# Ends of row blocks spread between messages, and GpSimd operations behind its gathers, in a two-layer graph kernel

## The chip, the cores and the metric

The kernel runs on one core of a Trainium2 chip. The metric is the device time of one execution in microseconds (us). Each core has five engines with queues of their own: TensorE (PE in the profile, its weight loads PEld), VectorE (DVE), ScalarE (ACT), GpSimd (POOL) and SyncE (SP), which here only issues transfers. Each engine runs its queue in order.

## The reference

The input is a feature matrix `x` (2708 x 128), an adjacency matrix `adj` (2708 x 2708, mostly zeros, rows normalised), and small weights. Two layers follow each other, each as `x = layernorm(x + layer(x))`.

```python
# layer 0, cut to what matters
XW = mobius_matvec(W, x)                      # x @ W, rescaled per row
gamma = 2 / max(1 - |XW|^2, eps)
two_mean = (adj @ (gamma * XW)) / (adj @ (gamma - 1))
# ... scalings per row, relu, then x = layernorm(x + ...)

# layer 1
s = x @ msg_w[:, :D].T
d = x @ msg_w[:, D:].T
messages = gelu(s[:, None, :] + d[None, :, :] + msg_b)
aggregated = einsum('ijd,ij->id', messages, adj)
new = concat([x, aggregated]) @ upd_w.T + upd_b
h = gelu(new) + x
x = layernorm(x + layernorm(h) * ln_w + ln_b)
```

## The kernel before, in words

The rows are cut into 22 blocks of 128. Layer 0 reads `adj` block by block, multiplies it on TensorE (L324), and finds at the same time where each row has its nonzero entries: ScalarE takes signs (L319), TensorE and VectorE turn them into keys and lists (L350, L358, `extract`). The nonzero entries of all rows of a block are packed into tiles of 128 edges: 99 tiles over 25 lists (block 0 has four). For each tile, one indirect transfer issued by GpSimd gathers the 128 values of `adj` into a column of `V` (L452, through the helper at L191). Its list of addresses `F` comes from a pool with three buffers (L430), written by VectorE at L448.

After layer 0, `layer0_end` computes the new `x` for blocks 0 to 15 and then 16 to 21, and writes the product `d` of layer 1 into a table in device memory (L535).

Layer 1 works only on the edges. For a tile of 128 edges, `messages` issues one indirect transfer that gathers 128 rows of the table (L651, again L191), repeats the row's `s` with a matmul against a selection matrix `R` (L652), builds `rv`, a 128x128 matrix with the values of `V` at each edge's row, on VectorE (L654), adds (L657), applies gelu on ScalarE (L658), and multiplies by `rv` on TensorE into the sum of the block (L660). Up to four tiles form a quad, which shares one buffer `dd` (a ring of seven) and one of three buffers `rv`.

Tiles are "early" if all their rows lie in the first 16 blocks of the table, and otherwise "late"; 62 are early (`soon`), 37 late. For blocks 0 to 7 the early tiles go first, as far as they fit into the ring, then into the buffer `aT` that layer 0 no longer needs; their sums are kept. Then all blocks follow in five groups, `GROUPS = [(0, 8), (8, 6), (14, 4), (18, 2), (20, 2)]`, with the remaining tiles. Each block ends with a copy of its sum (L702) and `update` (three or four matmuls into `sel` and a gelu, L610 to L614). After a group's last block, `finish` takes the whole group: add of `x1` (L618), statistics of each block (L594, L595), inverse root (L224 to L229 on VectorE, or one pow on GpSimd at L604 for the last group), scaling on ScalarE (L627), two wide VectorE operations (L628, L629), statistics again, scaling on ScalarE (L635) and a store for each block (L637).

The order of instructions within each engine is set by a planner, from the order of the program, dependences, and hints: `tc.issue_after(ins)` asks that what stands under it be put behind an instruction.

Of the kernel before, what the change touches and what calls it, by code (L numbers as in the profile page):

```python
# [10 lines left out]
F32 = mybir.dt.float32  # L11
# [3 lines left out]
AF = mybir.ActivationFunctionType  # L15
OP = mybir.AluOpType
AX = mybir.AxisListType

P = 128
# [3 lines left out]
LN_EPS = 1e-5  # L23
# [5 lines left out]
EARLY = 8  # L29
# [4 lines left out]
SPLIT = 16  # L34
# [41 lines left out]
def hyperbolic_then_message_kernel(  # L76
# [22 lines left out]
    const = ctx.enter_context(tc.tile_pool(name="const", bufs=1))  # L99
# [7 lines left out]
    w0_sb, wT, rowvec, o = pk[:, :D], pk[:, D : 5 * D].rearrange("p (i d) -> p i d", d=D), {}, 5 * D  # L107
# [27 lines left out]
    iotaN = const.tile([P, P], F32, name="iotaN")  # L135
# [51 lines left out]

    of_block = {b: [l for l, v in enumerate(LISTS) if v[0] == b] for b in range(NB)}

    def gather(o, src, at):  # L190
        nc.gpsimd.indirect_dma_start(  # L191
            out=o, out_offset=None, in_=src, in_offset=bass.IndirectOffsetOnAxis(ap=at, axis=0)
        )

    mx = big.tile([P, NB, D], F32, name="mx")
    y = big.tile([P, NB, D + 2], F32, name="y")
# [15 lines left out]
    def cols(n):  # L212
        count[0] += 1
        return sc.tile([P, n], F32, name=f"c{count[0]}")
# [49 lines left out]
    edge = ctx.enter_context(tc.tile_pool(name="edge", bufs=2))  # L264
    fin = ctx.enter_context(tc.tile_pool(name="fin", bufs=2))
# [5 lines left out]
    for g, n in quads:  # L271
# [18 lines left out]
    a, th, u, v, c = (cols(NB) for _ in range(5))  # L290
# [163 lines left out]
    x1, x1T = x_sb, xT  # L454
# [85 lines left out]
    last = {}  # L540
# [38 lines left out]
    gd = nom  # L579
# [10 lines left out]
    def moments(v, n, pool):  # L590
        st = pool.tile([P, n, 6], F32, name="st1")
        mv = pool.tile([P, n, 2], F32, name="mv1")
        for k in range(n):
            nc.vector.bn_stats(st[:, k, :], v[:, k, :])  # L594
            nc.vector.bn_aggr(mv[:, k, :], st[:, k, :])  # L595
        ve = pool.tile([P, n], F32, name="ve1")
        nc.vector.tensor_scalar_add(ve, mv[:, :, 1], LN_EPS)
        return mv, ve

    def inverse_root(ve, n, pool, last):  # L600
        if not last:
# [5 lines left out]
    def update(h, k, b, ags):  # L607
        up = bank("sel", 1)
        s = slice(b * P, (b + 1) * P)
        nc.tensor.matmul(up[:, :D], lhsT=x1T[:, s], rhs=wT[:, 2, :], start=True, stop=False)  # L610
        for ag in ags:
            nc.tensor.matmul(up[:, :D], lhsT=ag, rhs=wT[:, 3, :], start=False, stop=False)  # L612
        nc.tensor.matmul(up[:, :D], lhsT=ones[0:1, :], rhs=rowvec["ub"][0:1, :], start=False, stop=True)  # L613
        nc.scalar.activation(h[:, k, :], up[:, :D], AF.Gelu)  # L614

    def finish(h, b0, n, pool, last):

        nc.vector.tensor_add(h, h, x1[:, b0 : b0 + n, :])  # L618
        mv, ve = moments(h, n, pool)
        rs = inverse_root(ve, n, pool, last)  # L620
        nb = pool.tile([P, n], F32, name="nb")
        nc.vector.scalar_tensor_tensor(nb, mv[:, :, 0], -1.0, rs, op0=OP.mult, op1=OP.mult)
        for k0 in range(0, n, 4):
            k1 = min(n, k0 + 4)
            v = h[:, k0:k1, :]
            for k in range(k0, k1):
                nc.scalar.activation(h[:, k, :], h[:, k, :], AF.Identity, scale=rs[:, k : k + 1], bias=nb[:, k : k + 1])  # L627
            nc.vector.tensor_mul(v, v, wide(rowvec["lw"], k1 - k0))  # L628
            nc.vector.tensor_add(v, v, xlb[:, b0 + k0 : b0 + k1, :D])  # L629
        mv, ve = moments(h, n, pool)  # L630
        rs = inverse_root(ve, n, pool, last)
        nb = pool.tile([P, n], F32, name="nb")
        nc.vector.scalar_tensor_tensor(nb, mv[:, :, 0], -1.0, rs, op0=OP.mult, op1=OP.mult)
        for k in range(n):
            nc.scalar.activation(h[:, k, :], h[:, k, :], AF.Identity, scale=rs[:, k : k + 1], bias=nb[:, k : k + 1])  # L635
            r = rows[b0 + k]
            nc.sync.dma_start(out[(b0 + k) * P : (b0 + k) * P + r, :], h[:r, k, :])  # L637

    def ring(w):
        return edge.tile([P, 4, P], F32, name="dd", bufs=RING)[:, :w, :]  # L640

    def messages(b, ag, tiles, first, final, bins, room=ring):

        for q, k0 in enumerate(range(0, len(tiles), 4)):
            ts = tiles[k0 : k0 + 4]
            w = len(ts)
            dd = room(w)
            X = bank(bins[q % len(bins)]).rearrange("p (t d) -> p t d", d=D)[:, :w, :]
            rv = edge.tile([P, 4, P], F32, name="rv", bufs=3)
            for k, t in enumerate(ts):  # L650
                gather(dd[:, k, :], table[: SPLIT * P] if t in soon else table, J[:, t : t + 1])  # L651
                nc.tensor.matmul(X[:, k, :], lhsT=R[:, t, :], rhs=s_nm[:, b, :], start=True, stop=True)  # L652

                nc.vector.tensor_scalar(  # L654
                    rv[:, k, :], iotaN, rid[:, t : t + 1], V[:, t : t + 1], op0=OP.is_equal, op1=OP.mult
                )
            nc.vector.tensor_tensor(dd, X, dd, op=OP.add)  # L657
            nc.scalar.activation(dd, dd, AF.Gelu)  # L658
            for k in range(w):
                nc.tensor.matmul(  # L660
                    ag[:, :P],
                    lhsT=dd[:, k, :],
                    rhs=rv[:, k, :],
                    start=(first and k0 == 0 and k == 0),
                    stop=(final and k0 + k == len(tiles) - 1),
                )

    def own(b, ag):
        nc.tensor.matmul(ag[:, :P], lhsT=gd[:, b, :D], rhs=ident, start=True, stop=False)

    early, late, soon = {}, {}, set()
# [15 lines left out]
    for b in range(EARLY):  # L687
        ag = bank("ag", 1)
# [3 lines left out]
    for g0, gn in GROUPS:  # L692
        h = gd[:, g0 : g0 + gn, :D]
        for b in range(g0, g0 + gn):
            ag = bank("mp")
            agT = edge.tile([P, P], F32, name="agT")
# [29 lines left out]
    for i, v in enumerate(seconds):  # L726
        k = v.shape[1]
# [32 lines left out]
    with tc.If(dense > 0):  # L760
        with tc.tile_pool(name="dn", bufs=1) as dn:
            room = R.rearrange("p t i -> p (t i)")
            dT, sT, agT, row = (room[:, k * NP : (k + 1) * NP] for k in range(4))
            ge = flat(mx)
            nc.vector.memset(agT, 0.0)
            for c0 in range(0, NP, 512):
                c1_ = min(NP, c0 + 512)
                dp = bank("mp")
                nc.tensor.matmul(dp[:, : c1_ - c0], lhsT=wT[:, 1, :], rhs=x1T[:, c0:c1_], start=True, stop=True)
                nc.vector.tensor_copy(dT[:, c0:c1_], dp[:, : c1_ - c0])  # L770
                sp = bank("kx")
                nc.tensor.matmul(sp[:, : c1_ - c0], lhsT=wT[:, 0, :], rhs=x1T[:, c0:c1_], start=True, stop=True)
                nc.vector.tensor_scalar_add(sT[:, c0:c1_], sp[:, : c1_ - c0], mb)
            with tc.For_i(0, N, 1) as i:
                nc.sync.dma_start(row[:, :N], adj[bass.ds(i, 1), :].to_broadcast([P, N]))
                nc.scalar.activation(ge[:, :N], dT[:, :N], AF.Gelu, bias=sT[:, bass.ds(i, 1)])
                nc.vector.tensor_mul(ge[:, :N], ge[:, :N], row[:, :N])
                nc.vector.tensor_reduce(agT[:, bass.ds(i, 1)], ge[:, :N], axis=AX.X, op=OP.add)
            for b in range(NB):
                h = dn.tile([P, 1, D], F32, name="h")  # L780
                update(h, 0, b, [agT[:, b * P : (b + 1) * P]])
                finish(h, b, 1, dn, last=False)


_INS = [
# [73 lines left out]
```

## Time and profile before

| | |
|---|---|
| median of nine runs | 389.37 us (388.19 to 392.37) |
| the profiled execution, as timed | 390.27 us |
| its span in the profile | 388.5 us |
| TensorE busy | 300.3 us, 77% |
| VectorE busy | 277.7 us, 71% |
| ScalarE busy | 208.4 us, 54% |
| GpSimd busy | 204.9 us, 53% |
| mean granted TensorE clock | 0.867 |

The median is over separate runs; every duration comes from the one profiled execution, whose time is 0.9 us above the median and 1.8 us above its own span. In the page, a line of a group gives the source line, engine, operation, output and inputs, the count, the busy time in us, the mean of one in ns, and behind the second bar the idle time of the engine just before them with what ended most of it. L191 is the line of the helper that issues every gather, for values and for table rows alike.

### The profile page before, as it was taken

How to read it: one execution, taken by the hardware profiler on the slowest of the kernel's cores; microseconds unless marked ns; L12 is line 12 of the kernel's file. 1: busy time of each engine (PE TensorE's matmuls, PEld its weight loads, DVE VectorE, ACT ScalarE, POOL GpSimd, SP SyncE). 2: the span in 40 equal slices, each digit the busy share in tenths (PEclk: the TensorE clock that was granted, in tenths of full speed). 3: DMA queues.
4: the chain of work that ended last, by engine and by line, in shares of the span. 5: the costliest groups of instructions: out<-in, count | busy, mean ns of one | idle time of the engine just before them, and what ended most of it. 6: DMA issues, size and time to landing. Idle time of an engine off the chain costs nothing.

```text
span 388.5 us, 7784 instructions
## 1 busy us (share of the span) xinstructions
PE 300.3 (77%) x2427; PEld 271.9 (70%) x2427; DVE 277.7 (71%) x1474; ACT 208.4 (54%) x562; POOL 204.9 (53%) x297
## 2 busy tenths in 40 slices
PE   2519999999999999999799820759979995976300
PEld 2418999999999999999678720559869874865200
DVE  0996988887776677799958887399734656668650
ACT  2861857677667667689348632293323252273430
POOL 7400077777777444333320777777777777771000
PEclk9956999999999999999799955769968996899555
DMA  8800744434456546544426111212221222240110
GB/s 304 353 2 2 270 163 139 177 150 151 151 189 232 178 162 225 214 150 151 149 58 201 29 36 47 73 49 56 53 56 49 57 50 47 54 107 16 42 42 12
DMA packets 16237, 45.14 MB, mean 116 GB/s; under 512 B 5626, under 2 KB 11150, under 8 KB 13374
## 3 DMA queue, kind: packets, MB, share of 16 engines
q1 hardware_dynamic: 9710, 37.43, 26.6%
q0 software_dynamic: 6336, 6.55, 7.7%
q10 hardware_dynamic: 144, 0.60, 0.5%
q8 instruction: 20, 0.33, 0.3%
q14 instruction: 27, 0.22, 0.2%
HBM read 41.74 MB, written 2.83 MB: 115 GB/s over the span
## 4 chain that ended last, share of the span: by engine, by line
PE 56%; DVE 21%; ACT 10%; DMA 6%; issue 4%; POOL 2%; DVEq 0%; POOLq 0%; ACTq 0%
PE mp L324 23%; PE sel L438 6%; PE kx L350 6%; DMA dd<-table_dram,J 3%; PE mp L660 3%; PE X L528 3%; PE X L652 3%; POOL dd L191 2%; PE sel L612 2%; ACT sgn L319 2%; PE sel L613 2%; DVE rv L654 2%; PE kx L344 2%; DMA xT<-in_x_t_dram 2%; DVE dd L657 1%
## 5 line engine op out<-in xcount | busy, mean ns | idle before, releaser
L191 POOL DMA_INDIRECT V<-in_adj_dram,F x99 | 95.7, 966 | 101.2 <-DVE top L358 31.4
L324 PE MATMUL mp<-y,aT 128*128 128x130 f32 x968 | 123.3, 282 | 0.9 <-DVE y L308 0.9
L324 PEld LDWEIGHTS mp<-y,aT 128*128 128x128 f32 x968 | 115.8, 194 | 1.4 <-DVE y L308 1.1
L191 POOL DMA_INDIRECT dd<-table_dram,J x81 | 79.3, 979 | 35.4 <-issue 19.5
L319 ACT ACTIVATE sgn<-aT 128x2816 bf16<-128x2816 f32 x22 | 56.0, 2547 | 7.7 <-ACT junk L332 7.3
L652 PE MATMUL X<-mx,R 128*128 128x128 f32 x198 | 34.6, 308 | 15.0 <-DVE dd L657 12.7
L652 PEld LDWEIGHTS X<-mx,R 128*128 128x128 f32 x198 | 29.1, 214 | 17.8 <-DVE dd L657 14.1
L350 PEld LDWEIGHTS <-sgn 128*128 128x128 bf16 x484 | 28.7, 100 | 17.5 <-issue 9.1
L350 PE MATMUL kx<-kd,sgn 128*128 128x128 bf16 x484 | 34.0, 222 | 7.5 <-ACT sgn L319 7.5
L654 DVE TENSOR_SCALAR rv<-iotaN,rid,V 128x128 f32<-128x128 f32 x99 | 30.7, 364 | 9.0 <-PE mp L660 8.3
L438 PE MATMUL sel<-z,R 128*128 128x49 f32 (+4 forms) x198 | 29.2, 284 | 6.9 <-DVE z L429 2.6
L438 PEld LDWEIGHTS sel<-z,R 128*128 128x128 f32 x198 | 26.1, 199 | 9.0 <-DVE z L429 2.8
L358 DVE MAX8 top<-kx 128x8 f32<-128x128 f32 (+3 forms) x152 | 28.6, 236 | 2.9 <-PE kx L350 2.5
L409 ACT ACTIVATE work<-iota,mid 128x512 f32<-128x512 f32 (+3 forms) x53 | 26.8, 553 | 3.7 <-DVE mid L402 3.6
L657 DVE TENSOR_TENSOR dd<-X,dd 128x384 f32<-128x384 f32 (+3 forms) x29 | 15.1, 525 | 19.1 <-DMA dd<-table_dram,J 12.4
L658 ACT ACTIVATE dd<-dd 128x384 f32<-128x384 f32 (+3 forms) x29 | 13.8, 497 | 23.8 <-DVE dd L657 21.9
L660 PE MATMUL mp<-rv,dd 128*128 128x128 f32 x116 | 21.4, 317 | 4.0 <-ACT dd L658 4.0
L441 DVE TENSOR_TENSOR work<-sel,place 128x144 f32<-128x144 f32 (+11 forms) x29 | 11.7, 404 | 16.4 <-PE sel L438 16.1
L660 PEld LDWEIGHTS mp<-rv,dd 128*128 128x128 f32 x116 | 17.3, 217 | 6.3 <-ACT dd L658 5.1
L191 POOL DMA_INDIRECT aT<-table_dram,J x18 | 17.1, 950 | 5.5 <-issue 4.6
L362 ACT ACTIVATE junk_s<-kx 128x512 bf16<-128x512 f32 (+2 forms) x25 | 14.0, 562 | 8.8 <-DVE top L358 6.8
L614 ACT ACTIVATE nom<-sel 128x128 f32<-128x128 f32 x22 | 6.0, 274 | 20.4 <-PE sel L613 20.2
(204 smaller groups left out, 569.9 us busy)
## 6 DMA issues: line engine op xcount, KB each, us to landing
aT<-in_adj_t_dram SPq DMA_DIRECT2D x22, 1408.0 KB, 6.8
V<-in_adj_dram,F POOLq DMA_INDIRECT x99
xT<-in_x_t_dram SPq DMA_DIRECT2D x2, 704.0 KB, 7.2
x_sb<-in_x_nm_dram SPq DMA_DIRECT2D x2, 704.0 KB, 8.4
out_dram<-nom SPq DMA_DIRECT2D x21, 64.0 KB, 1.8
dd<-table_dram,J POOLq DMA_INDIRECT x81
table_dram<-dt SPq DMA_DIRECT2D x5, 256.0 KB, 2.3
pk<-in_pack_dram ACTq DMA_DIRECT2D x1, 587.5 KB
```

What stands on the lines that cost most here:

```text
L191: nc.gpsimd.indirect_dma_start(out=o, out_offset=None, in_=src, in_offset=bass.IndirectOffsetOnAxis(ap=at, axis=0))
L319: nc.scalar.activation(sgn, aT, AF.Sign, accum_out=signs[:, b : b + 1])
L324: nc.tensor.matmul(op[:, : D + 2], lhsT=aT[:, j, :], rhs=y[:, j, :], start=(j == 0), stop=(j == NB - 1))
L350: nc.tensor.matmul(kp[:, i * P : (i + 1) * P], lhsT=sgn[:, j, :], rhs=kd[:, q, :], start=False, stop=(i == len(groups) - 1 and j == j1 - 1),)
L358: nc.vector.max(top[:, c : c + 8], seg[:, s, :])
L362: nc.scalar.activation(t[:, :w], kp[:, :w], AF.Sign, accum_out=poss[:, l : l + 1])
L409: nc.scalar.activation(r0, iota[:, k0 * P : k1 * P], AF.Abs, scale=2.0, bias=mid[:, k : k + 1])
L438: nc.tensor.matmul(sp[:, k, :], lhsT=R[:, t0 + k0 + k, :], rhs=z, start=True, stop=True)
L652: nc.tensor.matmul(X[:, k, :], lhsT=R[:, t, :], rhs=s_nm[:, b, :], start=True, stop=True)
L654: nc.vector.tensor_scalar(rv[:, k, :], iotaN, rid[:, t : t + 1], V[:, t : t + 1], op0=OP.is_equal, op1=OP.mult)
L657: nc.vector.tensor_tensor(dd, X, dd, op=OP.add)
L660: nc.tensor.matmul(ag[:, :P], lhsT=dd[:, k, :], rhs=rv[:, k, :], start=(first and k0 == 0 and k == 0), stop=(final and k0 + k == len(tiles ...
```

## The change

Four things are changed, in layer 1 and in the helper for gathers.

The end of a row block is cut into parts. `node`, `first` and `finish` are now generators, and `messages` calls `step` at the end of each quad, which takes every waiting block one part further. The first statistics are taken for each block as soon as it is updated (`first`), and no longer for the group.

The first norm is written as two VectorE operations for each block, each doing two steps, where ScalarE did one operation and VectorE two wide ones. In the last group the second norm's scaling is a VectorE operation too.

Behind each gather of a `V` column and of an early tile, GpSimd raises a column of ones to a constant power and writes it into a scratch column `gap`, which nothing reads.

For late tiles, GpSimd builds `rv` itself, behind the tile's gather, where VectorE did.

The diff, without the part that serves a path not taken here:

```diff
+    gap = const.tile([P, 1], F32, name="gap")
+
+    def gather(o, src, at, wait=True):
+        last = nc.gpsimd.indirect_dma_start(
             out=o, out_offset=None, in_=src, in_offset=bass.IndirectOffsetOnAxis(ap=at, axis=0)
         )
+        if wait:
+            with tc.issue_after(last.ins):
+                nc.gpsimd.tensor_tensor(gap, ones[:, :1], nhalf, op=OP.pow)
+        return last
...
     def finish(h, b0, n, pool, last):
-        nc.vector.tensor_add(h, h, x1[:, b0 : b0 + n, :])
-        mv, ve = moments(h, n, pool)
+        mv = mvs.pop(b0)
+        ve = pool.tile([P, n], F32, name="ve1")
+        nc.vector.tensor_scalar_add(ve, mv[:, :, 1], LN_EPS)
         rs = inverse_root(ve, n, pool, last)
-        nb = pool.tile([P, n], F32, name="nb")
-        nc.vector.scalar_tensor_tensor(nb, mv[:, :, 0], -1.0, rs, op0=OP.mult, op1=OP.mult)
-        for k0 in range(0, n, 4):
-            k1 = min(n, k0 + 4)
-            v = h[:, k0:k1, :]
-            for k in range(k0, k1):
-                nc.scalar.activation(h[:, k, :], h[:, k, :], AF.Identity, scale=rs[:, k : k + 1], bias=nb[:, k : k + 1])
-            nc.vector.tensor_mul(v, v, wide(rowvec["lw"], k1 - k0))
-            nc.vector.tensor_add(v, v, xlb[:, b0 + k0 : b0 + k1, :D])
-        mv, ve = moments(h, n, pool)
+        yield
+        st = pool.tile([P, n, 6], F32, name="st1")
+        mw = pool.tile([P, n, 2], F32, name="mv1")
+        for k in range(n):
+            v = h[:, k, :]
+            nc.vector.scalar_tensor_tensor(v, v, mv[:, k, 0:1], rowvec["lw"], op0=OP.subtract, op1=OP.mult)
+            nc.vector.scalar_tensor_tensor(v, v, rs[:, k : k + 1], xlb[:, b0 + k, :D], op0=OP.mult, op1=OP.add)
+            moments(h, st, mw, [k])
+            if k % 2 and k + 1 < n:
+                yield
+        ve = pool.tile([P, n], F32, name="ve1")
+        nc.vector.tensor_scalar_add(ve, mw[:, :, 1], LN_EPS)
+        yield
         rs = inverse_root(ve, n, pool, last)
...
         for k in range(n):
+            v, r = h[:, k, :], rows[b0 + k]
+            if last:
+                nc.vector.tensor_scalar(v, v, mw[:, k, 0:1], rs[:, k : k + 1], op0=OP.subtract, op1=OP.mult)
+            else:
+                nc.scalar.activation(v, v, AF.Identity, scale=rs[:, k : k + 1], bias=nb[:, k : k + 1])
             nc.sync.dma_start(out[(b0 + k) * P : (b0 + k) * P + r, :], h[:r, k, :])
...
+    def first(h, b0, n, pool, k):
+        if k == 0:
+            mvs[b0] = pool.tile([P, n, 2], F32, name="mv0")
+        st = pool.tile([P, 1, 6], F32, name="st0")
+        nc.vector.tensor_add(h[:, k, :], h[:, k, :], x1[:, b0 + k, :])
+        moments(h, st, mvs[b0], [k], k)
+
+    def node(h, k, b, b0, n, ag, more, pool):
+        agT = edge.tile([P, P], F32, name="agT")
+        nc.scalar.copy(agT, ag[:, :P])
+        yield
+        update(h, k, b, [agT, *more])
+        yield
+        first(h, b0, n, pool, k)
+        if k == n - 1:
+            yield
+            yield from finish(h, b0, n, pool, last=(b == NB - 1))
+
+    queue = []
+
+    def step():
+        for g in list(queue):
+            if next(g, queue) is queue:
+                queue.remove(g)
...
-                gather(dd[:, k, :], table[: SPLIT * P] if t in soon else table, J[:, t : t + 1])
+                g = gather(dd[:, k, :], table[: SPLIT * P] if t in soon else table, J[:, t : t + 1], t in soon)
                 nc.tensor.matmul(X[:, k, :], lhsT=R[:, t, :], rhs=s_nm[:, b, :], start=True, stop=True)
-                nc.vector.tensor_scalar(
-                    rv[:, k, :], iotaN, rid[:, t : t + 1], V[:, t : t + 1], op0=OP.is_equal, op1=OP.mult
-                )
+                args = rv[:, k, :], iotaN, rid[:, t : t + 1], V[:, t : t + 1]
+                if t in soon:
+                    nc.vector.tensor_scalar(*args, op0=OP.is_equal, op1=OP.mult)
+                else:
+                    with tc.issue_after(g.ins):
+                        nc.gpsimd.tensor_scalar(*args, op0=OP.is_equal, op1=OP.mult)
...
+            step()
...
-            nc.scalar.copy(agT, ag[:, :P])
-            update(h, b - g0, b, [agT, gd[:, b, :D]] if b < EARLY else [agT])
-        finish(h, g0, gn, fin, last=(g0 + gn == NB))
+            queue.append(node(h, b - g0, b, g0, gn, ag, [gd[:, b, :D]] if b < EARLY else [], fin))
+    while queue:
+        step()
```

More of the change, by code (lines that the diff above doesn't have):

```diff
@@ L188, in hyperbolic_then_message_kernel @@
     of_block = {b: [l for l, v in enumerate(LISTS) if v[0] == b] for b in range(NB)}
-    def gather(o, src, at):
-        nc.gpsimd.indirect_dma_start(
+    gap = const.tile([P, 1], F32, name="gap")
+    def gather(o, src, at, wait=True):
+        last = nc.gpsimd.indirect_dma_start(
             out=o, out_offset=None, in_=src, in_offset=bass.IndirectOffsetOnAxis(ap=at, axis=0)
         )
+        if wait:
+            with tc.issue_after(last.ins):
+                nc.gpsimd.tensor_tensor(gap, ones[:, :1], nhalf, op=OP.pow)
+        return last
     mx = big.tile([P, NB, D], F32, name="mx")
@@ L588, in hyperbolic_then_message_kernel, with moments @@
         nc.vector.tensor_add(xlb[:, g : g + n, :D], x1[:, g : g + n, :], wide(rowvec["lb"], n))
[L590 to L598, printed above, removed]
+    def moments(v, st, mv, ks, k0=0):
+        for k in ks:
+            nc.vector.bn_stats(st[:, k - k0, :], v[:, k, :])
+            nc.vector.bn_aggr(mv[:, k, :], st[:, k - k0, :])
     def inverse_root(ve, n, pool, last):
@@ L631, in finish @@
+        ve = pool.tile([P, n], F32, name="ve1")
+        nc.vector.tensor_scalar_add(ve, mw[:, :, 1], LN_EPS)
+        yield
         rs = inverse_root(ve, n, pool, last)
-        nb = pool.tile([P, n], F32, name="nb")
-        nc.vector.scalar_tensor_tensor(nb, mv[:, :, 0], -1.0, rs, op0=OP.mult, op1=OP.mult)
+        if not last:
+            nb = pool.tile([P, n], F32, name="nb")
+            nc.vector.scalar_tensor_tensor(nb, mw[:, :, 0], -1.0, rs, op0=OP.mult, op1=OP.mult)
         for k in range(n):
-            nc.scalar.activation(h[:, k, :], h[:, k, :], AF.Identity, scale=rs[:, k : k + 1], bias=nb[:, k : k + 1])
-            r = rows[b0 + k]
-            nc.sync.dma_start(out[(b0 + k) * P : (b0 + k) * P + r, :], h[:r, k, :])
+            v, r = h[:, k, :], rows[b0 + k]
[3 more added lines that the diff above has]
+                nc.scalar.activation(v, v, AF.Identity, scale=rs[:, k : k + 1], bias=nb[:, k : k + 1])
+            nc.sync.dma_start(out[(b0 + k) * P : (b0 + k) * P + r, :], h[:r, k, :])
@@ new lines, in finish @@
+        yield
+    mvs = {}
+    def first(h, b0, n, pool, k):
[12 more added lines that the diff above has]
+        if k == n - 1:
+            yield
+            yield from finish(h, b0, n, pool, last=(b == NB - 1))
@@ L695, in hyperbolic_then_message_kernel @@
             ag = bank("mp")
-            agT = edge.tile([P, P], F32, name="agT")
             if b < EARLY:
@@ L781, in hyperbolic_then_message_kernel @@
                 update(h, 0, b, [agT[:, b * P : (b + 1) * P]])
-                finish(h, b, 1, dn, last=False)
+                first(h, b, 1, dn, 0)
+                for _ in finish(h, b, 1, dn, last=False):
+                    pass
 _INS = [
```

## The prediction, made before the changed kernel had run

> **What bounds the kernel now.** I read the page first (slices and costliest groups), then the timeline of GpSimd, the table of stretches, and last the chain of waits of the final 15 us.
>
> The page, slices and groups:
>
> ```profile
> DVE  0996988887776677799958887399734656668650
> POOL 7400077777777444333320777777777777771000
> L191 POOL DMA_INDIRECT V<-in_adj_dram,F x99 | 95.7, 966 | 101.2 <-DVE top L358 31.4
> L191 POOL DMA_INDIRECT dd<-table_dram,J x81 | 79.3, 979 | 35.4 <-issue 19.5
> ```
>
> GpSimd shows one digit, 7, in slices 23 to 36 (213.7 to 349.7 us). A constant share below full is the sign of a fixed pitch. The timeline of GpSimd (start, duration, in brackets the idle time before) confirms it, and shows where the row of gathers ends:
>
> ```profile
> 347.62 0.95 POOL L191 DMA_INDIRECT dd<-table_dram,J  x1 [0.30 <-ACT dd L658]
> 348.87 0.94 POOL L191 DMA_INDIRECT dd<-table_dram,J  x1 [0.30 <-issue]
> 350.12 0.94 POOL L191 DMA_INDIRECT dd<-table_dram,J  x1 [0.30 <-ACT nom L614]
> 373.68 0.73 POOL L604 TENSOR_TENSOR ro<-ve,nhalf 128x2 f32<-128x2 f32 x1 [22.62 <-DVE ro L225]
> 379.31 0.70 POOL L604 TENSOR_TENSOR ro<-ve,nhalf 128x2 f32<-128x2 f32 x1 [4.89 <-DVE ve L597]
> ```
>
> A gather starts every 1.25 us (0.94 plus 0.30), whatever it moves. From 213.5 to 351.06 us there are 108 of them (9 of V, 99 of table rows) with never more than about 0.3 us between them. So GpSimd's queue sets the moment T = 351.06 us at which the last gather is issued; any GpSimd time put ahead of it moves T one for one. The span ends at 388.5: the **tail** behind T is 37.4 us. In it GpSimd and TensorE idle, and VectorE and ScalarE hand the norms to each other:
>
> ```profile
> core 0: us, PE busy (x) PEld busy (x) DVE busy (x) ACT busy (x) POOL busy (x), PEclk, DMA share, GB/s
> 345.00:355.00 10.00, 8.24 (x54) 6.59 (x53) 7.15 (x27) 5.07 (x16) 4.71 (x5) 1.00 0.25 51
> 355.00:365.00 10.00, 4.37 (x22) 3.16 (x20) 6.84 (x44) 5.11 (x16) 0.00 (x0) 0.75 0.14 41
> 365.00:375.00 10.00, 1.01 (x4) 0.93 (x4) 7.50 (x61) 2.86 (x8) 0.73 (x1) 0.50 0.10 28
> 375.00:389.00 14.00, 0.00 (x0) 0.00 (x0) 2.44 (x12) 2.52 (x6) 0.70 (x1) 0.50 0.06 18
> ```
>
> The last add of messages (L657) ends at 357.75, the last norm (L635) at 381.17; 7.3 us of stores and ending follow. So the tail is 6.7 + 23.4 + 7.3.
>
> **What the Trainium skill says.** *Perfetto Trace Analysis*, DMA Instruction — SWDGE: the end shown for a gather is when the last DSP has written its descriptors, and the DSP completes the instruction after that. That leaves open what the 0.30 us is: completion of the gather (then any operation behind it waits too), or the start of the next gather (then something else fits there). The trace has no operation directly behind a gather. The same page (GPSIMD Engine Instruction) advises timing by start-to-start spacing; the 1.25 us is such a spacing. *GPSIMD Engine Reference*, 2.1 Instruction dispatch: completion needs all eight cores, and a core goes to the next instruction once its own share is done. *SBUF — State Buffer*, Who interferes with whom: a VectorE operation with two SBUF inputs contends with a GpSimd one that reads SBUF. No slowing shows in the trace: the add of one 128x256 pair at L628 takes 0.42 to 0.43 us both at 351 us among gathers and at 371 us without.
>
> **The change, part by part.**
>
> 1. *The tail.* Norms of earlier blocks no longer stand behind each other at the end, and 22 ScalarE operations (L627, 479 ns) go. But by the built order VectorE still has 105 instructions behind its last message add, because groups 14-17, 18-19 and 20-21 finish there. By rows of before: 57 small ones at 0.10 (25 such took 2.4 us from 366.68 to 369.1) is 5.7; 12 pairs of statistics at 0.26 is 3.1; 4 adds at 0.28 is 1.1; 14 of the new two-operation norm at 0.29 (between L334, 283 ns, and L328, 345 ns) is 4.1; 2 last scalings at 0.3 is 0.6. Together 14.6, plus one pow round through GpSimd, 0.9 (379.17 to 380.04). The last data lands 2.5 to 3.75 us behind its issue, so about T+2.6 (data of four gathers in the chain of waits); the eight `rv` that GpSimd now builds behind the last gather take 8 x 0.30 = 2.4 and are there as well. End at T + 2.6 + 15.5 + 7.3 = T + 25.4 instead of T + 37.4: **-12.0**. Bounds -6 (five blocks wait for those `rv`, and TensorE needs some eight matmuls for each, 0.43 at half clock and 0.22 at full in the chain of waits, so up to 17 us instead of 9) and -16 (part of VectorE's work done while it waits).
> 2. *VectorE relieved.* 37 `rv` at 364 ns leave it, 13.5 us between 283 and 349 us. VectorE is busy 3 to 8 of every 10 us there; the gathers cover this. Counted as 0.
> 3. *GpSimd's scratch columns and `rv`.* By the built order there are, from the first row gather on, still 108 gathers, 71 scratch columns, and 29 `rv` ahead of the last gather. They stand in 56 places between gathers, 43 beginning with a scratch column and 13 with an `rv`. One place holds 24 columns: the 23 gathers issued ahead of the `aT` ones have their columns put behind the eighteenth `aT` gather, and not "behind each". Prices: an `rv` is one 128x128 two-step scalar operation, 0.30 (the page's L136). A column has no row. From below 0.09 (a one-column memset, L185); 0.19 is the one-column L148; from above 0.70 (the two-column pow, L604). I take 0.19, and that the operation lies in the 0.30:
>    - 43 places: 0.94 + 0.19 instead of 1.25, -0.11 each: -4.7 (a gain is not excluded).
>    - 13 places: 0.94 + 0.30, about 0.
>    - 23 further columns of the lump, 0.19: +4.4, with nothing to hide them.
>    - 21 further operations in runs, 16 `rv` at 0.30 and 5 columns at 0.19: +5.7.
>    - Sum on T: **+5.4**. From below, -8 (a column at 0.09); from above, with 0.30 kept and 0.70 paid, 71 x 0.70 + 29 x 0.38 = +61.
> 4. *Columns behind the 90 V gathers of layer 0.* The queue there runs full from 48 to 126 us at 1.25, then waits for VectorE. A slower pitch is covered until a buffer fails: `F` has three, so the list of block 11 writes `F` (143 us) only when the gathers of block 8 are through. Sixty-one gathers from 48 us on end at 48 + 61 x pitch: at 1.13, 117 us, cost 0; the cover is gone above a pitch of 1.55.
> 5. *New waits.* An `rv` on GpSimd waits for TensorE to release one of three buffers; gathers queue behind it. In before VectorE waited so 6 times, 8.3 us. By the order 14 gathers stand ahead of the first ten `rv`, so the release is old by then: 0, at most +8. SP's queue gets the same 22 stores.
>
> Sum: -12.0 + 5.4 = -6.6. The profiled execution took 390.27 us around its span of 388.5; that gives 383.7. It stood 0.9 us above the median of the runs shown, 389.37, so **382.8 us**, 1.7% less.
>
> **Rivals.**
>
> *The column is paid in part (slower).* If pow needs 0.5 for one column (two take 0.70) and the 0.30 only makes room for part: 43 x 0.19 + 23 x 0.5 + 16 x 0.30 + 5 x 0.5 = 27, less 12, is +15: 404. For it: pow is the only one of GpSimd's small operations with 0.7 us. It decides from about 0.3 us a column, where 43 places cost nothing won and the lump costs 7.
>
> *Paid in full (slower still).* The 0.30 belongs to the gather's own completion; pitch 0.94 + 0.30 + 0.5 = 1.74: 71 x 0.5 + 29 x 0.38 = 46, layer 0 waits for `F` until 154 us instead of 143, +11; less 12: 435. For it: the 0.30 follows every gather, with a semaphore wait or without.
>
> *A gather with another operation behind it ends sooner.* 56 gathers shorter by a further 0.30: T 17 us earlier, but TensorE is busy 85 of the 100 us from 255 to 355, so at most 14 of it: 368. Against it: a gather with 2.5 us of nothing behind it also shows 0.94.
>
> *It doesn't do what it says.* The planner already lumps 24 columns; if only the tail's -12 and a lump of like size remain, 389.
>
> **How the numbers follow.** A measurement of this kernel tells about 0.5% from no change. The columns fit: 0.40, own range 374 to 391 (0.31 faster, 0.06 same, 0.03 slower). Sooner ends: 0.20, faster. Paid in part: 0.25, 391 to 412, slower. Paid in full: 0.13, 412 to 460, slower. Nothing left: 0.02. Faster 0.51, same 0.08, slower 0.41. The range 364 to 412 leaves out the full price and the best of the sooner ends, some 0.18.
>
> **What would show it.** In the profile after: start-to-start from a gather over its column to the next gather (1.13 right, 1.25 neutral, 1.4 or more wrong); the lump of 24 (4.6 us or 12); the start of the last gather against 350.12; the time from it to the end (25 or 37); the gathers of layer 0 (end of the full stretch near 117 to 126 us, or waits of VectorE's L448). The forecast is wrong if the columns take 0.3 us or more each.

## The result, and the profile after

The changed kernel takes 471.1 us (median of 10 runs, 470.1 to 475.9), the kernel before 389.8 us (31 runs, 388.2 to 392.8): ratio **1.211**, 95% interval 1.208 to 1.215. It is slower by 81 us where 7 us less were forecast, and it lies above the stated range of 364 to 412 us. Runs that came out more than 1.5% above the fastest of their kernel are left out of the times from here on, except in the part on the two sets in which the kernel before takes 500 us.

The profiled execution took 472.39 us around a span of 470.7 us. The page of the changed kernel, slices and groups, in the same form as that of the kernel before:

```profile
DVE  1998888633547669996887497310013443343792
POOL 5300888889888888835278788888798888888300
...
L193 POOL DMA_INDIRECT V<-in_adj_dram,F x99 | 99.3, 1003 | 59.9 <-DVE top L364 30.1
L198 POOL TENSOR_TENSOR gap<-ones,nhalf 128x1 f32<-128x1 f32 x161 | 97.0, 602 | 5.8
L193 POOL DMA_INDIRECT dd<-table_dram,J x81 | 81.0, 1000 | 29.1 <-issue 18.8
...
L699 POOL TENSOR_SCALAR rv<-iotaN,rid,V 128x128 f32<-128x128 f32 x37 | 29.4, 802 | 3.6 <-PE mp L703 3.0
...
L454 DVE SCALAR_TENSOR_TENSOR F<-J,rid 128x3 uint32<-128x3 uint32 (+5 forms) x29 | 4.7, 163 | 27.4 <-DMA V<-in_adj_dram,F 19.5
```

GpSimd's 7s have become 8s and 9s, and its second costliest group is the column that nothing reads: 161 of them, 97.0 us. An `rv` costs GpSimd 802 ns on average. VectorE now waits 19.5 us for gathers of `V` before it can write `F` (0.2 us before). The chain that ended last, shares by engine and by line:

```profile
POOL 34%; PE 34%; DVE 15%; issue 8%; ACT 4%; DMA 3%; POOLq 0%; DVEq 0%; ACTq 0%
PE mp L330 14%; POOL gap L198 11%; POOL dd L193 10%; POOL V L193 5%; POOL rv L699 4%; PE sel L444 4%; POOL aT L193 4%; PE kx L356 4%; PE X L534 3%; PE mp L703 2%; DMA V<-in_adj_dram,F 1%; DMA xT<-in_x_t_dram 1%; PE sel L614 1%; ACT sgn L325 1%; PE kx L281 1%
```

GpSimd's share was 2% before. The timeline of GpSimd (start, duration, idle time before in brackets), first where columns stand between gathers, then the lump:

```profile
304.23 0.99 POOL L193 DMA_INDIRECT aT<-table_dram,J  x1 [0.17 <-issue]
305.25 0.58 POOL L198 TENSOR_TENSOR gap<-ones,nhalf 128x1 f32<-128x1 f32 x1
306.01 0.99 POOL L193 DMA_INDIRECT aT<-table_dram,J  x1 [0.18 <-issue]
...
310.60 15.02 POOL L198 TENSOR_TENSOR gap<-ones,nhalf 128x1 f32<-128x1 f32 x24
325.87 1.00 POOL L193 DMA_INDIRECT dd<-table_dram,J  x1 [0.25 <-issue]
```

From gather to gather over a column it is 1.78 us and not 1.25: 0.99 for the gather, 0.03, 0.58 for the column, 0.18. And at the end of the row of gathers:

```profile
430.49 0.99 POOL L193 DMA_INDIRECT dd<-table_dram,J  x1 [0.17 <-issue]
431.53 0.82 POOL L699 TENSOR_SCALAR rv<-iotaN,rid,V 128x128 f32<-128x128 f32 x1
432.52 1.03 POOL L193 DMA_INDIRECT dd<-table_dram,J  x1 [0.17 <-issue]
433.60 5.58 POOL L699 TENSOR_SCALAR rv<-iotaN,rid,V 128x128 f32<-128x128 f32 x7
442.15 0.79 POOL L699 TENSOR_SCALAR rv<-iotaN,rid,V 128x128 f32<-128x128 f32 x1 [2.98 <-PE mp L703]
```

The last gather ends at T = 433.55 (432.52 + 1.03). The last message add, on VectorE:

```profile
446.33 0.29 DVE L700 TENSOR_TENSOR dd<-X,dd 128x128 f32<-128x128 f32 x1 [0.55 <-PE X L692]
```

The first gather of table rows, in the kernel before and in the changed one:

```profile
213.50 0.94 POOL L191 DMA_INDIRECT dd<-table_dram,J  x1 [11.03 <-DMA table_dram<-dt]
232.57 1.01 POOL L193 DMA_INDIRECT dd<-table_dram,J  x1 [8.91 <-DMA table_dram<-dt]
```

Three differences add up to the whole of the span's 82.2 us:

| stretch | before | after | difference | predicted |
|---|---|---|---|---|
| start to first gather of table rows | 213.50 | 232.57 | +19.1 | 0 |
| from there to T | 137.6 | 201.0 | +63.4 | +5.4 |
| T to the end of the span | 37.4 | 37.1 | -0.3 | -12.0 |

By the rows above, the 63.4 are 47 columns at 0.53 (25), the lump (15), and 29 `rv` at 0.80 (23).

### The profile page after: what moved, and what is told of

It is laid out like the page before. It is cut to its first block, busy times and chain, and to the rows that moved or that the text cites. A ratio compares the mean times of both kernels' runs of the same rounds, so it can differ in the third digit from the quotient of the medians.

```text
span 470.7 us, 7986 instructions
## 1 busy us (share of the span) xinstructions
PE 328.8 (70%) x2427; PEld 295.9 (63%) x2427; DVE 274.0 (58%) x1480; ACT 200.0 (42%) x538; POOL 337.3 (72%) x495
## 4 chain that ended last, share of the span: by engine, by line
POOL 34%; PE 34%; DVE 15%; issue 8%; ACT 4%; DMA 3%; POOLq 0%; DVEq 0%; ACTq 0%
PE mp L330 14%; POOL gap L198 11%; POOL dd L193 10%; POOL V L193 5%; POOL rv L699 4%; PE sel L444 4%; POOL aT L193 4%; PE kx L356 4%; PE X L534 3%; PE mp L703 2%; DMA V<-in_adj_dram,F 1%; DMA xT<-in_x_t_dram 1%; PE sel L614 1%; ACT sgn L325 1%; PE kx L281 1%
## 5 line engine op out<-in xcount | busy, mean ns | idle before, releaser
L193 POOL DMA_INDIRECT V<-in_adj_dram,F x99 | 99.3, 1003 | 59.9 <-DVE top L364 30.1
L198 POOL TENSOR_TENSOR gap<-ones,nhalf 128x1 f32<-128x1 f32 x161 | 97.0, 602 | 5.8
L692 PE MATMUL X<-mx,R 128*128 128x128 f32 x198 | 42.2, 358 | 30.8 <-DVE dd L700 21.8
L692 PEld LDWEIGHTS X<-mx,R 128*128 128x128 f32 x198 | 36.2, 260 | 33.9 <-DVE dd L700 22.4
L703 PE MATMUL mp<-rv,dd 128*128 128x128 f32 x116 | 28.5, 378 | 33.1 <-POOL rv L699 32.3
L703 PEld LDWEIGHTS mp<-rv,dd 128*128 128x128 f32 x116 | 22.6, 265 | 37.3 <-POOL rv L699 37.0
L699 POOL TENSOR_SCALAR rv<-iotaN,rid,V 128x128 f32<-128x128 f32 x37 | 29.4, 802 | 3.6 <-PE mp L703 3.0
L662 ACT COPY agT<-mp 128x128 f32<-128x128 f32 x22 | 5.9, 266 | 60.3 <-PE mp L703 53.8
L696 DVE TENSOR_SCALAR rv<-iotaN,rid,V 128x128 f32<-128x128 f32 x62 | 18.9, 356 | 16.0 <-PE mp L703 16.0
L454 DVE SCALAR_TENSOR_TENSOR F<-J,rid 128x3 uint32<-128x3 uint32 (+5 forms) x29 | 4.7, 163 | 27.4 <-DMA V<-in_adj_dram,F 19.5
```

The costliest lines, as they stand in the source:

```text
L193: last = nc.gpsimd.indirect_dma_start(out=o, out_offset=None, in_=src, in_offset=bass.IndirectOffsetOnAxis(ap=at, axis=0))
L198: nc.gpsimd.tensor_tensor(gap, ones[:, :1], nhalf, op=OP.pow)
L696: nc.vector.tensor_scalar(*args, op0=OP.is_equal, op1=OP.mult)
L699: nc.gpsimd.tensor_scalar(*args, op0=OP.is_equal, op1=OP.mult)
L703: nc.tensor.matmul(ag[:, :P], lhsT=dd[:, k, :], rhs=rv[:, k, :], start=(first and k0 == 0 and k == 0), stop=(final and k0 + k == len(tiles ...
```

## The experiments

**Theory A:** from the first gather of table rows on GpSimd's queue is full, so each operation ahead of the last gather is paid at its own length, less what fits into the 0.30 us between two gathers; and in layer 0 the longer pitch makes VectorE wait for a buffer of `F`. **Rivals:** B, the place between gathers costs, whatever stands there; C, the ends in parts cost the time; D, the lower TensorE clock (0.793 for 0.867) does.

In two sets of runs the kernel before, run beside the others, took about 500 us and not 390. Their times are not set against those of the other sets; they stand at the end of this section.

### Columns and rv, taken out one at a time

e1, no columns: `-        if wait:` / `+        if False:` in `gather`.

> Only the scratch columns are left out; late rv stay on GpSimd. Theory A (each GpSimd operation ahead of the last gather is paid in full, because GpSimd's queue is full): layer 0 as in the kernel before, first row gather near 213.5; 29 rv at 0.80 = 23 us in the stretch from there to the last gather, so that starts near 351 + 23 = 374 (370 if an rv lies in the 0.30 between two gathers); behind it the eight late rv again, so about 37 to the end: 408 to 412 us. Theory B (an operation that stands between gathers costs by its place, whatever it is; columns are only part of it): layer 0 as before, but rv places still stretched, over 425. Theory C (the ends in parts cost the time themselves): over 440. Theory D (the lower TensorE clock, 0.79 for 0.87, makes the kernel long): clock and time stay near those of the changed kernel, 460 to 470.

e2, no columns and every `rv` on VectorE, thus ends in parts and the new norm alone:

```diff
-                if t in soon:
-                    nc.vector.tensor_scalar(*args, op0=OP.is_equal, op1=OP.mult)
-                else:
-                    with tc.issue_after(g.ins):
-                        nc.gpsimd.tensor_scalar(*args, op0=OP.is_equal, op1=OP.mult)
+                nc.vector.tensor_scalar(*args, op0=OP.is_equal, op1=OP.mult)
```

> No columns, and every rv on VectorE: what is left of the change is the ends in parts and the first norm as two VectorE operations. Theory A: GpSimd's queue is again 108 gathers at 1.25 from 213.5, last one issued at 350 to 352; last add of messages 3 to 7 us later, 15 us of VectorE, 7 to 8 us of ending: 376 to 382 us (the -12 of the prediction's first step, seen alone). Theory C: 390 or more. Theory D: the clock stays at 0.79 and the time over 410.

e3, the column by another operation, `nc.gpsimd.memset(gap, 1.0)`:

> The scratch column is written by a memset and not by a power, at the same places; nothing reads it in either case. Theory A (the length of the operation is what costs): a memset of one column is 0.09 (L185 of before), between gathers 0.99 + 0.03 + 0.09 + 0.17 = 1.28 for 1.25; in layer 0 no wait for F; 48 places x 0.03 + 23 further in the lump x 0.11 = 4 us more than the kernel without columns: 411 to 416. Theory B (the place costs: a compute operation behind a gather makes the pitch 1.5 or more): 440 to 470.

e4, columns kept, every `rv` on VectorE by the diff of e2:

> Scratch columns as in the changed kernel, every rv on VectorE. Theory A: layer 0 stretched as in the changed kernel (first row gather near 232), lump of 24 columns 15 us, 29 rv x 0.80 = 23 us fewer up to the last gather: near 410 instead of 433.6; without rv behind it the last add of messages follows after 3 to 7 us instead of 13, then 16 and 8: 437 to 443 us. Rival for the tail (TensorE or the norms are late by themselves): the last gather near 410, but 37 us to the end again: 447 to 450.

Measured together (the kernel before: 389.95 us):

| kernel | us | ratio, 95% | first row gather | T | T to last message add | T to end |
|---|---|---|---|---|---|---|
| e1 no columns | 409.2 | 1.048 (1.041 to 1.055) | 212.1 | 370.9 | 12.5 | 36.1 |
| e2 ends only | 383.9 | 0.982 (0.976 to 0.989) | 212.9 | 349.5 | 5.4 | 33.6 |
| e3 memset column | 415.5 | 1.064 (1.056 to 1.071) | 212.9 | 375.9 | 14.6 | 38.6 |
| e4 rv on VectorE | 439.6 (of 437.1 and 442.1) | 1.127 (no interval) | 229.5 | 407.1 | 4.2 | 28.3 |

The times and ratios are over several runs, the four last columns come from one traced execution each. e4 scatters more than the others: its four runs took from 437.1 to 446.9 us.

Theory A's numbers hold in all but e2, which ended 2 us above its 376 to 382. C falls: ends in parts with the new norm are faster than before. D falls: the traced execution of e3 has a clock of 0.810 and takes 416.3 us, that of e4 a higher one, 0.837, and takes 437.1. Taking out columns is worth 471.1 - 409.2 = 62 us, and taking the `rv` off GpSimd then another 409.2 - 383.9 = 25. With the columns kept, the `rv` are worth 471.1 - 439.6 = 31.5. The two differ in the tail: there the `rv` cost 2.5 us without columns (36.1 for 33.6) and 8.8 us with them (37.1 for 28.3). From the first row gather to T, 29 `rv` cost 158.8 - 136.6 = 22.2 us (e1 against e2), 0.77 each.

e3 decides against B. Its timeline of GpSimd:

```profile
268.81 0.94 POOL L193 DMA_INDIRECT aT<-table_dram,J  x1 [0.19 <-issue]
269.75 0.11 POOL L198 MEMSET gap<- 128x1 f32 x1
270.06 0.94 POOL L193 DMA_INDIRECT aT<-table_dram,J  x1 [0.19 <-issue]
...
276.03 3.71 POOL L198 MEMSET gap<- 128x1 f32 x24
```

With an operation of 0.11 us in the same place the pitch is 1.25, as without one. The bubble does take in an operation of 0.11 us. Of a power of 0.58 us it took in 0.05, as the pitch rose by 0.53. The lump, where nothing hides it, is paid in full again: it is 3.7 of the 6.4 us by which e3 is above e1.

### What the columns of V do in layer 0

e5 is the kernel before with the column behind V gathers alone; e6 the same with a deeper pool:

```diff
-        F = small.tile([P, TMAX], U32, name="F", bufs=3)
+        F = small.tile([P, TMAX], U32, name="F", bufs=16)
```

> The kernel before, with one thing added: the power into a scratch column behind each V gather, none behind table rows; F keeps three buffers. Theory A (in layer 0 the slower pitch, 1.78 for 1.25, makes VectorE wait for a buffer of F, and that shifts all of layer 0): waits of VectorE's F line for V gathers of some 19 us, first row gather near 232 instead of 213.5, then 9 more V columns in layer 1 at 0.53 = 5: 412 to 415 us. Rival (prediction's step 4: the wait for lists covers it): first row gather stays near 213.5, 394 to 396.

> As the one before, with 16 buffers of F instead of three. Theory A: VectorE's wait for F is gone, the 90 gathers of layer 0 end near 48 + 90 x 1.78 = 208 or some us later by themselves, first row gather 213 to 218: 394 to 400 us. Rival (something else than F holds layer 0, such as GpSimd's memory accesses slowing VectorE): stays at 408 or more.

Beside those first runs the kernel before took about 500 us; the second ones count here.

> The kernel with columns behind V gathers alone once more, because its first time stood beside 502.9 us for the kernel before on that chip and not beside 390, so that it can't be set against the other runs. Where the kernel before takes 390: Theory A (VectorE waits for F) 412 to 415, first row gather near 232; rival (covered, the prediction's step 4) 394 to 396. Where it takes 500 again: 464 to 470.

> The same with 16 buffers of F once more, for the same reason. Where the kernel before takes 390: Theory A 394 to 400, first row gather 213 to 218, no wait for F; rival (something else than F holds layer 0) 408 or more. Where it takes 500 again: 447 to 449.

Measured beside 389.86 us: 415.4 us with three buffers, ratio 1.064 (1.060 to 1.068), first row gather at 235.3; 395.1 us with sixteen, ratio 1.014 (1.011 to 1.017), at 215.9 (in a traced execution of 402.1 us). VectorE's wait for `V` gathers at the line that writes `F` is 17.7 us in the first and 0.4 us in the second. Of the waits with three buffers by engine and line (us in total, times, longest), and of its timeline of GpSimd:

```profile
DVE F L453 <- DMA V<-in_adj_dram,F: 17.7, 3, 8.0
235.33 0.99 POOL L193 DMA_INDIRECT dd<-table_dram,J  x1 [9.46 <-DMA table_dram<-dt]
```

So 20 of 25 us are the buffer's; the 5.3 us left are about what 9 columns of layer 1 at 0.53 give (4.8).

e10 makes that one edit to the changed kernel, with eight buffers, and the order of instructions stays the same on every engine; e11 is the changed kernel unaltered.

> The changed kernel with eight buffers of F for three and nothing else; the order of instructions on every engine is the same. Theory A: VectorE's 19.5 us of waits for F go, first row gather near 213 to 218 instead of 232.6, what follows is unchanged: 452 to 457 us beside 471. Rival (the late V gathers only move the wait to the first rv of layer 1, or GpSimd is still behind with its 90 columns): 465 to 471.

> The changed kernel unaltered. Where the kernel before takes 390: 470 to 473. Where it takes 500, as it did beside the first run with columns behind V gathers: below that, 470 to 485, since a pitch of 1.78 leaves room that a pitch of 1.25 doesn't; rival: 82 us above it here too, 580.

Measured: 454.8 us (1.167, 1.162 to 1.171) and 471.5 us (1.210, 1.206 to 1.215). The same two rows of e10:

```profile
DVE F L454 <- DMA V<-in_adj_dram,F: 0.7, 3, 0.3
214.49 0.99 POOL L193 DMA_INDIRECT dd<-table_dram,J  x1 [1.98 <-DMA table_dram<-dt]
```

The wait is gone, the first row gather is back at 214.5, and from there to T it takes 200.1 us as in the changed kernel (201.0). So the stall for `F` is 17 us of the 81 inside the whole change, and 20 us with the `V` columns alone. (e11's trace has its first row gather at 229.4 where the changed kernel's first trace has 232.6, so single traces differ by some 3 us here.) Beside e11 the kernel before took 390.0 us, so how the changed kernel stands where that takes 500 was not measured.

### What an rv and a column cost by themselves

e12 is the kernel before with 28 GpSimd operations more, four of each form, ahead of the first gather.

```diff
+        nc.gpsimd.tensor_scalar(R[:, 0, :], iotaN, 3.0, 2.0, op0=OP.is_equal, op1=OP.mult)
+        nc.gpsimd.tensor_scalar(R[:, 1, :], iotaN, half, one, op0=OP.is_equal, op1=OP.mult)
+        nc.gpsimd.tensor_scalar(R[:, 2, :], iotaN, half, one, op0=OP.mult, op1=OP.add)
+        nc.gpsimd.tensor_scalar(R[:, 3, 0:1], iotaN[:, 0:1], half, one, op0=OP.is_equal, op1=OP.mult)
+        nc.gpsimd.tensor_tensor(R[:, 4, 0:1], one, half, op=OP.mult)
+        nc.gpsimd.tensor_tensor(R[:, 5, 0:1], one, half, op=OP.pow)
+        nc.gpsimd.tensor_tensor(R[:, 6, :], ones, iotaN, op=OP.mult)
```

> The kernel before with 28 GpSimd operations more ahead of the first gather, four of each of seven forms, into places of R that are written again later. Theory A (the form is what costs): 128x128 with two constants 0.30 as in L136 of before; the same with both values read from columns 0.75 to 0.80; one column with both values read from columns or by a multiplication 0.1 to 0.25; one column of power 0.58 to 0.63. Rival (the neighbourhood of gathers makes them dear): with columns 0.30 to 0.45, power 0.2 to 0.4. The whole stays near 390, GpSimd being idle there.

Its own lines in that order of the source, L192 to L202 (duration in ns: least, median, most):

```profile
L192 POOL TENSOR_SCALAR R<-iotaN x4: 637/659/675, 16.0 to 21.1; 128x128 f32<-128x128 f32 x4
L194 POOL TENSOR_SCALAR R<-iotaN,nhalf,ones x4: 789/794/823, 17.5 to 21.7; 128x128 f32<-128x128 f32 x4
L196 POOL TENSOR_SCALAR R<-iotaN,nhalf,ones x4: 452/459/477, 22.5 to 28.4; 128x128 f32<-128x128 f32 x4
...
L200 POOL TENSOR_TENSOR R<-ones,nhalf x4: 186/190/222, 23.4 to 29.2; 128x1 f32<-128x1 f32 x4
L202 POOL TENSOR_TENSOR R<-ones,nhalf x4: 561/568/583, 23.5 to 29.3; 128x1 f32<-128x1 f32 x4
```

This run is in one of the two sets in which the kernel before takes about 500 us; L136 takes 0.30 us in it too. The rival falls: away from any gather an `rv` is 0.79 and a column 0.57. But theory A had the cause of the first wrong. The same form with two constants is 0.66 and not 0.30, so it is above all the arithmetic that costs: with values from columns, multiply and add takes 0.46, comparison and multiply 0.79. Reading the values from columns adds 0.13 (0.66 to 0.79). The row that the prediction priced `rv` by, L136, is a multiply and add with constants. The cost of a column is the power's: the same one column by a multiply is 0.19, the very price that was taken. The multiplication of two 128x128 tiles (L204) is 0.45. One column by comparison and multiply (L198) is 0.41, so half of the 0.79 of an `rv` does not come from its width.

### The norm alone, and a version that beats both

e7 is the kernel before with the first norm rewritten and nothing else:

```diff
-                nc.scalar.activation(h[:, k, :], h[:, k, :], AF.Identity, scale=rs[:, k : k + 1], bias=nb[:, k : k + 1])
-            nc.vector.tensor_mul(v, v, wide(rowvec["lw"], k1 - k0))
-            nc.vector.tensor_add(v, v, xlb[:, b0 + k0 : b0 + k1, :D])
+                w = h[:, k, :]
+                nc.vector.scalar_tensor_tensor(w, w, mv[:, k, 0:1], rowvec["lw"], op0=OP.subtract, op1=OP.mult)
+                nc.vector.scalar_tensor_tensor(w, w, rs[:, k : k + 1], xlb[:, b0 + k, :D], op0=OP.mult, op1=OP.add)
```

> The kernel before with the first norm alone rewritten: two VectorE operations a block for one ScalarE and two wide VectorE operations, nothing in parts, no columns, rv on VectorE. Theory A (of the 6 us that ends in parts with this norm gained, the parts carry most): in the last group 2 scalings of 479 ns and their hand-overs go and some 0.3 us of VectorE come: 388 to 389.5 beside 390. Rival (the norm carries it): 384 to 386.

Measured 393.7 us, 1.009 (1.007 to 1.012): slower by 1%, outside what either side expected. VectorE's timeline shows where the norm stands:

```profile
357.96 1.66 DVE L626 SCALAR_TENSOR_TENSOR nom<-nom,ro,y 128x128 f32<-128x128 f32 x6
359.53 0.48 DVE L594 BATCH_NORM_STATS2 st<-nom 128x6 f32<-128x128 f32 x2
...
363.71 0.35 DVE L625 SCALAR_TENSOR_TENSOR nom<-nom,mv,pk 128x128 f32<-128x128 f32 x1
365.62 0.29 DVE L654 TENSOR_TENSOR dd<-X,dd 128x128 f32<-128x128 f32 x1
```

The norm of a group of six stands in one piece ahead of the last message add (L654), which comes 14.7 us behind the last gather and not 6.4 as before. Cut into parts (e2) it comes after 5.4 us. The span's end comes 41.5 us behind the last gather, 4 us later than before. So with the new norm in both, the parts gain 393.7 - 383.9 = 10 us, and the norm in one piece loses 4. Parts with the old norm were not run, and that the norm's place is the whole cause of its loss is read from the order, not tested.

In e2's tail VectorE waits for a buffer of the inverse root that six scalings on ScalarE still read. Two rows of its timeline, the last message add and that wait:

```profile
354.84 0.27 DVE L696 TENSOR_TENSOR dd<-X,dd 128x128 f32<-128x128 f32 x1
366.79 0.17 DVE L231 TENSOR_SCALAR ro<-rh 128x4 int32<-128x4 int32 x1 [2.88 <-ACT nom L645]
```

e8 is e2 with four buffers for `ro` and `nb` (the shift of a norm), and e9 besides takes the roots of the groups of 4 and 2 blocks by a power on GpSimd, as the last group does already (the line for `nb` is left out):

```diff
-            o = pool.tile([P, n], F32, name="ro")
+            o = pool.tile([P, n], F32, name="ro", bufs=4 if n > 1 else 1)
...
-        if not last:
+        if not last and n > 4:
             return rsqrt(ve, n, pool)
```

> Ends in parts alone (no columns, every rv on VectorE), with four buffers instead of two for the inverse root (ro) and the shift (nb) of the norms. In the tail of that kernel VectorE waits 2.9 us for ScalarE's six scalings (L645) that still read ro, and 2.8 us of ScalarE's for nb late by the same ring. Theory A: 2 to 4 us less than 383.9, so 380 to 382. Rival (VectorE's own work and TensorE's updates at half clock set the end; the wait only moves): 383 to 384.

> As the one before, and the roots of the groups of 4, 2 and 2 blocks by one power each on GpSimd, which is idle behind the last gather, instead of 11 small VectorE operations: about 40 small operations at 0.07 to 0.10 = 3 to 4 us leave VectorE in the tail, for four powers of 0.2 to 0.75 on another engine. Theory A (VectorE's work sets the tail): 377 to 380. Rival (hand-overs of 0.7 to 0.9 for each power, or TensorE's updates to 364 us, take it back): 381 to 384.

> Ends in parts with four buffers of ro and nb, and one power for each root of the groups of 4, 2 and 2 blocks, once more, for the same reason. Where the kernel before takes 390: Theory A (VectorE's work and the wait for ro set the tail) 377 to 380; rival (hand-overs or TensorE's updates take it back) 381 to 384. Where it takes 500 again: 487 to 492.

> Ends in parts alone with four buffers of ro and nb, once more, because its first time stood beside 502.9 us. Where the kernel before takes 390: Theory A (the wait of 2.9 us for ro sets the tail) 380 to 382, so that nearly all of the 3.4 us between the parts alone and the kernel with powers is the buffers; rival (VectorE's small operations set it) 383 to 384. Where it takes 500: 485 to 490.

e9b: **380.5 us** beside 389.86, ratio 0.976 (0.974 to 0.979), the fastest version: half a microsecond above theory A's range, below the rival's. T is 349.4 and the end of the span 28.8 us behind it. How much of the 3.4 us against e2 is the buffers' and how much the powers' stays open: both runs of e8 are in the sets in which the kernel before takes 500.

### The two sets in which the kernel before takes 500 us

The kernel before took 502.9 us (494.6 to 506.6, beside e5, e6, e8, e9) and 497.6 us (493.6 to 503.2, beside e12, e8b). Beside it e5 took 466.0 us (ratio 0.934, 0.924 to 0.943) and e6 448.2 (0.895, 0.887 to 0.903): there a column behind each `V` gather made the kernel faster, with three buffers of `F` and with sixteen. e8 took 489.3 (0.975, 0.968 to 0.983) and 484.7 (0.973, 0.968 to 0.979), e9 489.9 (0.979, 0.970 to 0.988), with no difference between the two; e12 took 499.7 (one run).

Some of the expectations take this for a property of the chip. That is not shown: the first of the two sets ran on the chip numbered 9, and so did e10 and e11, beside which the kernel before took 390.0 us (the second set ran on chip 5). What differs between the sets is not known. By the traces e6 gains in both layers: its first row gather is at 215.3 us and T comes 181 us later, against 255.0 and 193 in e12, which is the kernel before but for 28 early operations. The page of e9 from there (chain by engine) says no more than that engines wait for something that the profile doesn't name:

```profile
PE 38%; DVE 22%; another core or an unknown queue 15%; issue 11%; ACT 10%; DMA 2%; POOL 1%; DVEq 0%; POOLq 0%; ACTq 0%
```

Within a row of gathers the pitch stays 1.25 us there (e12). Why the other engines stand still beside them was not settled.

## Why the prediction was wrong, point by point

- **The bound** was right: GpSimd's queue sets T, and what is put ahead of T moves it. The count of 108 gathers, 71 columns with a lump of 24 and 29 `rv` was right as well.
- **Step 3, the columns**, failed by its price. "I take 0.19, and that the operation lies in the 0.30": the second half holds for what is short (e3: 0.11 us at the old pitch), the first does not. A column is a power of 0.58 to 0.60. The step's -4.7 and +4.4 and the five columns' 1.0 became 25 and 15, 40 us for 0.7. The text named the row against it itself, the pow of 0.70 us for two columns, and bounded the step at +61; the step with all its terms measured +63.4. That these two lie so close is chance: the bound has 0.70 for a column, which is too much, and 0.38 for an `rv`, which is too little.
- **Step 3, `rv`**: 0.30 from L136, for 0.77 to 0.80. L136 has the same shape and the same instruction name, but multiplies and adds; comparison and multiply take more than twice as long (e12). The 13 places priced 0 and the 16 `rv` priced 4.8 were 23 us.
- **Step 4** had the mechanism and the point from which it decides, "the cover is gone above a pitch of 1.55", and took 1.13. At 1.78 the stall is 17 us (e10) to 20 us (e5, e6); the prediction's own figure for 1.74 was 11. It looked at one list, at 143 us; the first long wait of the changed kernel, 7.9 us, ends at 113 us, and there are more.
- **Step 1, the tail**: -12.0 for -0.3. The term that failed is that the last data lands at "about T+2.6" and that the eight `rv` by then "are there as well": the last message add is at T + 12.8, and it waits 0.55 us for TensorE. TensorE had waited for an `rv` until 432.4 (1.75 us) and then works without a gap until 446; the eight `rv` behind the last gather take 0.8 each, and their last waits 3 us for TensorE in turn. This is what the step's bound of -6 was for, and it came out worse. With every `rv` on VectorE and the columns kept, the add is at T + 4.2 and the tail 28.3 (e4). The other terms were near: 15.5 us of VectorE's work behind the last add measured 16.2 us, and the ending 8.2 for 7.3. In e2, where T is early, VectorE needs 20.4 us behind the add, with a wait of 1.05 us for the gelu of an update, whose matmuls run at a clock of 0.50 there, and the wait of 2.88 us for `ro`: the tail is only 3.8 us shorter.
- **Step 2** (VectorE relieved, 0) was right: with every `rv` back on VectorE, e4 takes 177.6 us from the first row gather to T, which is the 137.6 of before and the 40 of the columns.
- **Step 5** (new waits, 0, at most +8): GpSimd waits 3.0 us for TensorE, as small as said. The wait the other way round, TensorE for `rv` from GpSimd, is 32.3 us in ten places and was not in the step. All of it lies ahead of T, where GpSimd's queue sets the pace anyhow; what it left was work for TensorE behind T.
- **The rivals**: paid in full, with its pitch of 1.74 and the wait for `F`, is nearest to what happened, but 471 lies above its range of 412 to 460 too. It gave 435 because it kept -12 for the tail, took an `rv` at 0.38 and the wait for `F` at 11 us. Its reason, that the 0.30 belongs to the gather's own completion, does not hold: the memset of e3 fits into it. It was given 0.13.
- **A reading**: the prediction saw no slowing of VectorE beside gathers, from L628 at 351 us. L628 is a multiply and not an add, and that one starts at 351.13, when the last gather has ended (351.06), so the comparison says nothing on the question.

## What to carry to other kernels

Before work is put on a queue that sets the end, price it by a row with the same operation, not only the same shape: between two kinds of arithmetic with constants on the same tile lay a factor of 2.2 here (0.66 to 0.30). For the column there was such a row, the power of two columns at 0.70, and it was nearer to the measured 0.58 than the multiply of one column at 0.19. Where no such row exists and the two bounds of a cost lie on different sides of the decision, the likeliest value deserves no more trust than the bounds. And a bubble between two instructions need not be free: of 0.30 us some 0.1 could be used here, and an operation of 0.58 us lengthened the pitch by 0.53.

## What the runs showed that was not expected

- On GpSimd a 128x128 comparison and multiply with constants takes 0.66 us, multiply and add 0.30 (L136); a power of a single column takes 0.57, a multiply of it 0.19.
- Of the 0.30 us between two gathers about 0.1 us can be used: with a memset of 0.11 us between them the pitch stays at 1.25, and with a longer operation 0.17 to 0.19 us remain ahead of the next gather.
- The same norm is slower in one piece (393.7 us) and faster in parts (383.9), where it no longer stands in one block ahead of the last message add.
- The kernel before takes 390 us in some sets of runs and about 500 in two others, and the effect of a column behind `V` gathers has the other sign there. What makes the difference stays open.
